# A linear-attention and mixture-of-experts kernel: one ordered attention block with its own beginning, shorter angle arithmetic, one power for two norms, scatters ahead of state sums, shared steps of the first sequence four tiles sooner

## The chip, the cores and the metric

The kernel runs on one core of a Trainium2 chip. The metric is the time of one execution on the device in microseconds (us). The engines are TensorE (PE, matrix products; PEld is its weight load), VectorE (DVE), ScalarE (ACT), GpSimd (POOL) and SyncE (SP, which issues most DMAs). Each engine takes its own instructions in order; they meet through semaphores.

## The reference

The input x has 16 sequences of 512 tokens of 128 features. Two layers follow each other, each with a residual and a layer norm behind it.

```
q, k, v = silu(x @ Wq), silu(x @ Wk), x @ Wv        # 16 heads of 8
q, k    = [t*cos(theta*n), t*sin(theta*n)]          # n is the position, per head
out     = ((q k^T) * lower_triangle) v              # no softmax
out     = (out @ Wo) * sigmoid(x @ G1 @ G2)
x       = layernorm(x + (layernorm of out)*gamma + beta)

probs   = softmax(rmsnorm(x) @ router^T)            # 8 experts, the best 2 of each token
routed  = sum over the 2 experts of w * (silu(xg @ rg) * (xg @ ru)) @ rd
          # an expert takes its first 1280 tokens in order
shared  = (silu(x @ sg) * (x @ su)) @ sd
x       = layernorm(x + shared + routed)
```

## The kernel before

**Tiles.** A tile is 128 tokens; there are 64, four to a sequence (NC = 4). Attention is done tile by tile with a running state per sequence, so a tile needs its own 128 by 128 energies and the state of the tiles before it.

**The beginning.** Positions come from iotas. The angles theta*n are reduced to whole turns in `angles` (L299 to L311, nine DVE instructions per chunk c): the number of turns is the product of `turns_of` and the position plus MAGIC (L304), MAGIC is taken off and the result multiplied with the two parts of two pi (L305, L308), and the difference is put together (L307, L309), its size taken (L310) and it is clamped (L311). `sines` (L316 to L326) has ACT take cosine and sine of a chunk in four instructions, into `cst_tok`; `same` (L331) copies half of it. The four chunks serve all sequences.

**One attention tile t.** `project` (L414): two products with the weights into a PSUM tile `pq`, three Silu on ACT into `qk` (L425, L427), a Tanh for the gate (L433), four ACT copies that spread the values into `vpad` (L441), and on DVE the product of `qk` with the sines, `hat` (L445). `turn_over` (L452): four transposes of `hat` on PE, and four ACT instructions that bring them back (L460, L465, L467). `energies` (L493): 32 products, masked by four DVE instructions (L513). `values` (L518): products with the state and the values; ACT brings the result to `oT` (L544). `remember` (L470): the products of keys and values, masked by DVE (L488), and added to the running state by POOL (L490). All their PSUM tiles but the energies are of one tag, "w", with four buffers.

**After a sequence.** `after(b)` (L547) is a generator: the output product, the gate, a layer norm, a residual, a second layer norm, the transpose into `x1T` and the router's logits. Its reciprocal roots are powers on POOL (L113 through `rstd_of`); L591 to L594 work out the reciprocal root for the router's norm from the second norm. `route(b0, b1)` (L618) is a generator over a group of sequences (0 to 5, 6 to 11, 12 to 15) of small DVE instructions, an Exp, two counting products, and it fills a list of 128 scatters. A scatter (L723) is an indirect DMA on POOL that writes the rows of one tile to an expert's slots. `scatter_behind` (L736) puts an optional small POOL product, `beat` (L740), ahead of it, which makes POOL wait for a given column.

**The shared network** is a list `feed` of 384 steps (`shared_order`, L182): per sequence 16 gate or up steps of one product of 512 columns each (L137, L150), and 8 down steps of four products (L160). A gate step has a Silu on ACT (L139), an up step a product on DVE (L151), every second down step a sum on DVE (L165). A sequence's steps may start when `ready[b]` allows.

**What sets the order.** Blocks under `tc.manual_schedule(engines=ORDERED)` keep the written order on PE, ACT, DVE and POOL. Before, there are three such blocks in the attention phase: the set-up (L217), the first angles with the masks (L333), and the main loop (L788). Each keeps its own order, and the scheduler interleaves them. The main loop runs t from -2 to 64; in each pass it does `project(t+2)`, a shared step, some steps of `route`, `turn_over(t+1)`, a shared step, a step of `after`, `energies(t)`, `values(t-1)`, `remember(t+1)`, two scatters, and more steps of `after` and `route`. `beginning(t)` (L389) puts the later angles and sines ahead of `project`. A tail loop follows with one shared step per pass and a scatter in every second one. Then come the experts (L999), and a final loop (L1047 to L1066), which takes a shared step per pass, and beside it sums the experts' rows (`add_up`, every second pass) and deals out steps of the last layer norm (`finish_lot`, three steps for two passes), in lots of four tiles, and of one tile for the last four. When the shared steps are used up, what is left of these runs by itself.

Of the kernel before, what the change touches and what calls it, by code (L numbers as in the profile page):

```python
# [10 lines left out]
F32 = mybir.dt.float32  # L11
I32 = mybir.dt.int32
AF = mybir.ActivationFunctionType
ALU = mybir.AluOpType
# [33 lines left out]
def tile_kernel(  # L48
# [44 lines left out]
    rms = keep.tile([P, NT], F32, name="rms")  # L93
# [101 lines left out]
    with ExitStack() as ph:  # L195
# [21 lines left out]
        with tc.manual_schedule(engines=ORDERED):  # L217
            th_row = cst.tile([1, D + HALF], F32, name="th_row")
            nc.sync.dma_start(th_row, theta.unsqueeze(0))
# [15 lines left out]
            nc.vector.memset(half_pi, math.pi / 2)  # L235
            warm = cst.tile([P, 1], F32, name="warm")
# [36 lines left out]
            for vp in vpads[:2]:  # L273
                nc.gpsimd.memset(vp, 0.0)

            def nought(tile_, n):
                nc.scalar.copy(tile_, zcol.to_broadcast([P, n]))

            pth = ps_w.tile([P, D + HALF], F32, tag="w", name="pth")
            nc.tensor.matmul(pth, ones[0:1, :], th_row, start=True, stop=True)  # L280
            th_sb = wk1.tile([P, D + HALF], F32, tag="w", name="th_sb")
            nc.scalar.copy(th_sb, pth)
# [3 lines left out]
            for vp in vpads[2:]:  # L286
                nought(vp.rearrange("p a b d -> p (a b d)"), 640)
# [3 lines left out]

            cst_tok = cst.tile([P, NC, 2, 16, 2, 8], F32, name="cst_tok")
            scratch = hp.tile([P, 10, D + HALF], F32, tag="h", name="scratch")
            turns_of = wk1.tile([P, D + HALF], F32, tag="o", name="turns_of")
            nc.vector.tensor_scalar(turns_of, pth, 1.0 / (2.0 * math.pi), None, ALU.mult)

        def angles(c, th):  # L299

            a, size, k, whole = scratch[:, c], scratch[:, NC + c], scratch[:, 8], scratch[:, 9]
            both = ((slice(0, D), pos[:, 0, c : c + 1]), (slice(D, D + HALF), pos[:, 1, c : c + 1]))
            for m, at in both:
                nc.vector.tensor_scalar(k[:, m], turns_of[:, m], at, MAGIC, ALU.mult, ALU.add)  # L304
            nc.vector.tensor_scalar(whole, k, MAGIC, -C1, ALU.subtract, ALU.mult)  # L305
            for m, at in both:
                nc.vector.scalar_tensor_tensor(a[:, m], th[:, m], at, whole[:, m], ALU.mult, ALU.add)  # L307
            nc.vector.tensor_scalar(k, k, MAGIC, -C2, ALU.subtract, ALU.mult)  # L308
            nc.vector.tensor_tensor(a, a, k, ALU.add)  # L309
            nc.vector.scalar_tensor_tensor(size, a, -1.0, a, ALU.mult, ALU.max)  # L310
            nc.vector.tensor_scalar(a, a, -PI_BELOW, PI_BELOW, ALU.max, ALU.min)  # L311
# [4 lines left out]
        def sines(c):  # L316

            for s, (from_, scale, bias) in enumerate([(scratch[:, NC + c], -1.0, half_pi), (scratch[:, c], 1.0, 0.0)]):
                nc.scalar.activation(
                    cst_tok[:, c, 0, :, s, :], from_[:, 0:D].rearrange("p (h d) -> p h d", d=8), AF.Sin,  # L320
                    scale=scale, bias=bias,
                )
                nc.scalar.activation(
                    by_twos(cst_tok[:, c, 1])[:, :, 1, :, s, :],
                    from_[:, D:].rearrange("p (a i d) -> p a i d", i=2, d=8), AF.Sin, scale=scale, bias=bias,
                )  # L326

        def same(c):

            to, of = (by_twos(cst_tok[:, c, a])[:, :, 0].rearrange("p a i s d -> p a (i s d)") for a in (1, 0))  # L330
            nc.vector.tensor_copy(to, of)  # L331

        with tc.manual_schedule(engines=ORDERED):  # L333
            angles(0, pth)
            sines(0)
            angles(1, th_sb)
            same(0)

# [3 lines left out]
            nc.gpsimd.tensor_tensor(causal[:, 0:1], scratch[:, 0, 0:1], zcol, ALU.mult)  # L342
# [13 lines left out]
            for at in (0, HALF):  # L356
                rows = causal[at : at + HALF, :]
                nc.gpsimd.affine_select(
                    rows, rows, pattern=[[1, HALF]], compare_op=ALU.is_ge, fill=0.0, base=0, channel_multiplier=-1
                )  # L360
            expi = cst.tile([P, E], I32, name="expi")
# [27 lines left out]
        def beginning(t):  # L389

            if t == -1:
                sines(1)
            elif t == 0:
                angles(2, th_sb)
                sines(2)
            elif t == 1:
                angles(3, th_sb)
                sines(3)

# [14 lines left out]
        def project(t):  # L414

            b, c = divmod(t, NC)
            pq = ps_w.tile([P, 16, 32], F32, tag="w", name=f"pq_{t}")
# [6 lines left out]
            qk = wk2.tile([P, 2 * D], F32, tag="qk", name=f"qk_{t}")  # L424
            nc.scalar.activation(qk[:, 0:D].rearrange("p (h d) -> p h d", d=8), pq[:, :, 0:8], AF.Silu)  # L425
            for u in range(2):
                nc.scalar.activation(  # L427
                    qk[:, D:].rearrange("p (a u i d) -> p a u i d", u=2, i=2, d=8)[:, :, u],
                    pq[:, 0:8, 16 + 8 * u : 24 + 8 * u].rearrange("p (a i) d -> p a i d", i=2), AF.Silu,
                )  # L430
            if c == 0:
                gates[b] = wk2.tile([P, NC, D], F32, tag="gate", name=f"gate_{b}")
# [3 lines left out]

            vp, v = vpads[t % NVP], pq[:, 8:16, 16:32].rearrange("p k (u d) -> p k u d", u=2)
# [4 lines left out]
            if 0 < t < NC:  # L442
                same(t)
# [103 lines left out]
        def after(b):  # L547
# [28 lines left out]
            r2 = rstd_of(mv2[:, :, 1], NC, LN_EPS)  # L576
# [12 lines left out]

            sq = small.tile([P, NC], F32, tag="sq", name="sq")  # L590
            nc.vector.tensor_tensor(sq, r2, r2, ALU.mult)  # L591
            nc.vector.tensor_tensor(sq, sq, mv2[:, :, 1], ALU.mult)
            nc.vector.tensor_scalar(sq, sq, RMS_EPS, None, ALU.add)
            nc.gpsimd.tensor_tensor(rms[:, mine], sq, neghalf[:, :NC], ALU.pow)  # L594
# [193 lines left out]
        with tc.manual_schedule(engines=ORDERED):  # L788
            for t in range(-2, NT + 1):
                coming, here, left = 0 <= t + 2 < NT, 0 <= t < NT, 0 <= t - 1 < NT  # L790
                stopped("wait")
                beginning(t)
# [5 lines left out]
                if t == 0:  # L798
                    nc.vector.tensor_scalar(wo_sb, wo_sb, 0.5, None, ALU.mult)
# [16 lines left out]
                if 0 <= t + 1 < NT:  # L816
                    remember(t + 1)
                if left:

                    scatter_behind(oTs[(t - 1) // NC][:, ds((t - 1) % NC * P, 1)])  # L820
                    scatter_behind()
                advance(turns, "narrow")
# [3 lines left out]
                if left and (t - 1) % NC == NC - 1:  # L826
                    b = (t - 1) // NC
                    turns.append(after(b))
                    ready[b] = t + (6 if b else 10)
                    for b0, b1 in groups:  # L830
                        if b == b1 - 1:
                            todo.append((b, route(b0, b1)))
# [5 lines left out]
            while turns or todo or scatters or fills or over:  # L838
# [17 lines left out]
                t += 1  # L856

# [255 lines left out]
```

## Time and profile before

| | us |
|---|---|
| median of 8 runs (lowest, highest) | 856.41 (854.03, 857.22) |
| the profiled execution | 852.86 |
| its span, first to last instruction | 851.2 |

| stretch of the span, us | what runs | PE busy |
|---|---|---|
| 9.53 to 35.86 | tiles 0 to 6 of attention | 19.96 of 26.33 |
| 80.55 to 102.64 | attention with shared steps | 22.09 of 22.09 |
| 355 to 510 | tail loop: shared steps and scatters | 152.94 of 155 |
| 510 to 750 | experts | 238.05 of 240 |
| 750 to 843 | final loop | 89.56 of 93 |
| 843 to 851.2 | the last layer norms alone | 0 |

Matrix products are pipelined, so a busy PE holds some waiting inside; the table shows where it stands still. The timeline of an engine gives for each group of instructions its start, its duration, and in brackets the time that the engine stood idle before it and what ended that time. The starts of L445, one per tile, mark the pace of the attention phase; "hat 6" in what follows is the seventh of them.

### The profile page before, as it was taken

The numbers are of one execution on the slowest core, as the hardware profiler recorded it, in microseconds if no ns is written. First come the engines' busy times: TensorE is split into PE (matmuls) and PEld (weight loads), VectorE is DVE, ScalarE is ACT, GpSimd is POOL, SyncE is SP. The second block draws the span as 40 slices with busy tenths as digits, with TensorE's granted clock in tenths as the row PEclk, the third lists the DMA queues.
The fourth block names the chain that finished last, engine by engine and source line by source line (L and its number), as shares of the span: only waits on it lengthen the run. The fifth ranks groups of instructions, "written<-read, shape, count | busy, mean of one in ns | idle before, by whom it ended". The sixth has DMA issues, their size and how long they took to land. (4 is left out here: it accounts for less than half of the span.)

```text
span 851.2 us, 25793 instructions
## 1 busy us (share of the span) xinstructions
PE 814.0 (96%) x10288; PEld 555.6 (65%) x10288; DVE 538.8 (63%) x1695; ACT 413.7 (49%) x1342; POOL 360.1 (42%) x512
## 2 busy tenths in 40 slices
PE   6899999989999999999999999999999999999995
PEld 4666667656766765755666666776777667765564
DVE  8688887889988788975433334443434443278864
ACT  5676776675676667434222221333333333323455
POOL 2233333322366767686766660433343333401110
PEclk9899999999999999999999999999999999999998
DMA  6011111111021110067000014212331110056412
GB/s 202 22 36 34 35 33 35 34 34 29 27 58 57 56 48 25 26 215 247 28 11 7 2 37 134 84 35 91 94 98 55 62 59 25 31 161 180 143 49 63
DMA packets 66395, 57.55 MB, mean 68 GB/s; under 512 B 6180, under 2 KB 55132, under 8 KB 66274
## 3 DMA queue, kind: packets, MB, share of 16 engines
q1 hardware_dynamic: 59474, 44.95, 17.3%
q0 software_dynamic: 6656, 10.69, 3.8%
q8 instruction: 81, 1.33, 0.7%
q14 instruction: 40, 0.33, 0.1%
q10 hardware_dynamic: 144, 0.26, 0.1%
HBM read 32.62 MB, written 26.48 MB: 69 GB/s over the span
## 5 line engine op out<-in xcount | busy, mean ns | idle before, releaser
L723 POOL DMA_INDIRECT xg_dram<-x,idx x128 | 128.6, 1004 | 40.4 <-issue 35.1
L934 POOL DMA_INDIRECT y_dram<-y,to x80 | 77.5, 969 | 158.2 <-ACT y L932 158.2
L151 DVE TENSOR_TENSOR h<-sl,pu 128x512 f32<-128x512 f32 x128 | 87.7, 685 | 84.5 <-PE pu L150 56.3
L139 ACT ACTIVATE sl<-pg 128x512 f32<-128x512 f32 x128 | 75.5, 593 | 118.1 <-PE pg L137 112.5
L150 PE MATMUL pu<-x1T,su_sb 128*128 128x512 f32 x256 | 131.0, 593 | 0.7 <-ACT sl L139 0.7
L137 PE MATMUL pg<-x1T,sg_sb 128*128 128x512 f32 x256 | 131.4, 595 | 0.0
L160 PE MATMUL pd<-sd_sb,h 128*128 128x128 f32 x1024 | 122.8, 276 | 4.4 <-DVE x1T L165 4.4
L1026 DVE TENSOR_TENSOR eh<-esl,peu 128x512 f32<-128x512 f32 (+1 forms) x96 | 57.5, 599 | 109.7 <-PE peu L1023 109.7
L160 PEld LDWEIGHTS pd<-sd_sb,h 128*128 128x128 f32 x1024 | 119.1, 192 | 11.3 <-issue 5.7
L113 POOL TENSOR_TENSOR rstd<-ve,neghalf 128x4 f32<-128x4 f32 x45 | 48.6, 1080 | 124.7 <-DVE ve L111 119.8
L928 PEld LDWEIGHTS ped<-rd,eh 128*128 128x128 f32 x640 | 84.1, 192 | 24.6 <-issue 22.5
L490 POOL TENSOR_TENSOR state<-state,add 128x128 f32<-128x128 f32 x96 | 44.0, 458 | 129.9 <-DVE add L488 127.3
L513 DVE TENSOR_TENSOR et<-pe,causal 128x256 f32<-128x256 f32 x256 | 90.4, 417 | 8.8 <-PE pe L505 8.7
L1021 PE MATMUL peg<-xgT,rg 128*128 128x512 f32 (+1 forms) x192 | 84.6, 523 | 0.0
L1023 PE MATMUL peu<-xgT,ru 128*128 128x512 f32 (+1 forms) x192 | 84.4, 521 | 0.0
L928 PE MATMUL ped<-rd,eh 128*128 128x128 f32 x640 | 84.4, 275 | 0.0
L1025 ACT ACTIVATE esl<-peg 128x512 f32<-128x512 f32 (+1 forms) x96 | 50.5, 526 | 55.0 <-PE peg L1021 52.3
L150 PEld LDWEIGHTS pu<-x1T,su_sb 128*128 128x128 f32 x256 | 45.8, 190 | 45.1 <-issue 39.0
L932 ACT ACTIVATE y<-ped,wt 128x128 f32<-128x128 f32 x80 | 29.4, 367 | 84.6 <-PE ped L928 84.6
L137 PEld LDWEIGHTS pg<-x1T,sg_sb 128*128 128x128 f32 x256 | 44.5, 191 | 36.8 <-issue 34.8
L418 PE MATMUL pq<-W,xT 128*128 128x384 f32 x128 | 61.0, 560 | 5.4 <-ACT qT L467 2.0
L445 DVE TENSOR_TENSOR hat<-qk,cst_tok 128x512 f32<-128x512 f32 x64 | 45.0, 703 | 25.8 <-ACT qk L427 25.7
(176 smaller groups left out, 1259.8 us busy)
## 6 DMA issues: line engine op xcount, KB each, us to landing
y_dram<-vpad SPq DMA_DIRECT2D x16, 512.0 KB, 7.0
y<-y_dram SPq DMA_DIRECT2D x32, 256.0 KB, 3.2
xT<-xt SPq DMA_DIRECT2D x15, 384.0 KB, 3.1
xg<-xg_dram SPq DMA_DIRECT2D x8, 660.0 KB, 4.4
x<-x SPq DMA_DIRECT2D x16, 256.0 KB, 3.4
o<-res SPq DMA_DIRECT2D x15, 256.0 KB, 2.3
xg_dram<-x,idx POOLq DMA_INDIRECT x128, 2.3
rg<-rg SPq DMA_DIRECT2D x8, 256.0 KB, 4.7
```

The lines of the kernel that those rows point to most:

```text
L137: nc.tensor.matmul(pg, sg_sb[:, ts(i, P)], seq, start=True, stop=True)
L139: nc.scalar.activation(sl, pg, AF.Silu)
L150: nc.tensor.matmul(pu, su_sb[:, ts(i, P)], seq, start=True, stop=True)
L151: nc.vector.tensor_tensor(h[i // half][:, i % half, :], h.pop(("s", i)), pu, ALU.mult)
L160: nc.tensor.matmul(pd, h[k][:, i - k * half, ts(c, P)], sd_sb[:, i, :], start=(i == 0), stop=(i == IS // P - 1))
L418: nc.tensor.matmul(pq[:, :, 0:24], xts[b][:, c, 0:P], W[:, 0:384].rearrange("p (h n) -> p h n", n=24), start=True, stop=True)
L513: nc.vector.tensor_tensor(et.rearrange("p s i n -> p (s i) n"), pes[a, half].rearrange("p s i n -> p (s i) n"), causal.unsqueeze(1).to_bro ...
L723: i = nc.gpsimd.indirect_dma_start(out=xg_dram[:, :], out_offset=bass.IndirectOffsetOnAxis(ap=idx[:, k, t : t + 1], axis=0), in_=x1[:, t, ...
L928: nc.tensor.matmul(pd, h[:, i, ts(c, P)], got[e][2][:, i, :], start=(i == 0), stop=(i == IR // P - 1))
L934: i = nc.gpsimd.indirect_dma_start(out=y_dram[:, :], out_offset=bass.IndirectOffsetOnAxis(ap=to[:, at : at + 1], axis=0), in_=y, in_offset ...
L1021: nc.tensor.matmul(pg[:, :n], rg_sb[:, ts(i, P)], xgTs[e][:, ds(o0, n)], start=True, stop=True)
L1023: nc.tensor.matmul(pu[:, :n], ru_sb[:, ts(i, P)], xgTs[e][:, ds(o0, n)], start=True, stop=True)
```

## The change

- **One ordered block.** The set-up, the first angles and the main loop are one ordered block. The work of tiles 0 to 2 is written out by hand, and the loop starts at t = 1. `project` is cut into `products`, `squash`, `gate`, `spread` and `turn`, so that these can be placed singly.
- **Angles.** The product of theta with the position goes to ACT (`linear`, eight instructions), the number of turns comes from a matrix product with a row of 1/(2 pi), and `angles` has six DVE instructions. The size is taken by ACT (Abs) at the head of `sines`.
- **Loads and memsets.** theta is loaded by ACT's queue ahead of the weights. Two of the four `vpad` tiles, which ACT filled with noughts, are cleared by DVE and by POOL.
- **Norms.** `after` works out both reciprocal roots by one power over eight columns.
- **Scatters** stand ahead of `remember` in the pass.
- **Shared steps** of sequence 0 may start at t = 10 instead of t = 14.

The diff, cut to its core:

```diff
-    rms = keep.tile([P, NT], F32, name="rms")
+    norms = keep.tile([P, 2, NT], F32, name="norms")
+    rms = norms[:, 1]
...
-        with tc.manual_schedule(engines=ORDERED):
+        ordered = ExitStack()
+        ordered.enter_context(tc.manual_schedule(engines=ORDERED))
+        if True:
             th_row = cst.tile([1, D + HALF], F32, name="th_row")
-            nc.sync.dma_start(th_row, theta.unsqueeze(0))
+            nc.scalar.dma_start(th_row, theta.unsqueeze(0))
...
+            by_turn = cst.tile([1, P], F32, name="by_turn")
+            nc.vector.memset(by_turn, 1.0 / (2.0 * math.pi))
...
+            nc.vector.memset(vpads[3], 0.0)
...
+            pth = ps_w.tile([P, 2, M], F32, tag="w", name="pth")
+            nc.tensor.matmul(pth[:, 0], ones[0:1, :], th_row, start=True, stop=True)
+            nc.tensor.matmul(pth[:, 1], by_turn, th_row, start=True, stop=True)
...
-            for vp in vpads[2:]:
-                nought(vp.rearrange("p a b d -> p (a b d)"), 640)
...
+            def linear(c):
+                for m, order in both:
+                    nc.scalar.activation(
+                        scratch[:, NC + c, m], pth[:, 0, m], AF.Copy, scale=pos[:, order, c : c + 1]
+                    )
+
+            linear(0)
+            linear(1)
+            nc.scalar.copy(turns_of, pth[:, 1])
...
+            for c in range(2, NC):
+                linear(c)
+
+        def angles(c, turns):
+
+            a, k = scratch[:, c], scratch[:, 8 + c % 2]
+            for m, order in both:
+                nc.vector.tensor_scalar(a[:, m], turns[:, m], pos[:, order, c : c + 1], MAGIC, ALU.mult, ALU.add)
+            nc.vector.tensor_scalar(k, a, MAGIC, None, ALU.subtract)
+            nc.vector.scalar_tensor_tensor(a, k, -C1, scratch[:, NC + c], ALU.mult, ALU.add)
+            nc.vector.scalar_tensor_tensor(a, k, -C2, a, ALU.mult, ALU.add)
+            nc.vector.tensor_scalar(k, a, -PI_BELOW, PI_BELOW, ALU.max, ALU.min)
...
         def sines(c):
+            nc.scalar.activation(scratch[:, NC + c], scratch[:, c], AF.Abs)
...
+            nc.gpsimd.memset(vpads[2], 0.0)
...
+            ve = small.tile([P, 2, NC], F32, tag="ve2", name="ve2")
+            nc.vector.tensor_scalar(ve[:, 0], mv2[:, :, 1], LN_EPS, None, ALU.add)
+            inv = small.tile([P, NC], F32, tag="sq", name="inv")
+            nc.vector.reciprocal(inv, ve[:, 0])
+            nc.vector.tensor_tensor(inv, inv, mv2[:, :, 1], ALU.mult)
+            nc.vector.tensor_scalar(ve[:, 1], inv, RMS_EPS, None, ALU.add)
+            nc.gpsimd.tensor_tensor(
+                norms[:, :, mine], ve, neghalf[:, : 2 * NC].rearrange("p (k c) -> p k c", k=2), ALU.pow
+            )
...
-            sq = small.tile([P, NC], F32, tag="sq", name="sq")
-            nc.vector.tensor_tensor(sq, r2, r2, ALU.mult)
-            nc.vector.tensor_tensor(sq, sq, mv2[:, :, 1], ALU.mult)
-            nc.vector.tensor_scalar(sq, sq, RMS_EPS, None, ALU.add)
-            nc.gpsimd.tensor_tensor(rms[:, mine], sq, neghalf[:, :NC], ALU.pow)
...
+            products(0)
+            products(1)
+            sines(0)
+            squash(0)
+            turn(0)
+            spread(0)
+            gate(0)
+            sines(1)
+            turn_over(0)
+            angles(2, turns_of)
+            remember(0)
+            squash(1)
+            turn(1)
+            spread(1)
+            gate(1)
+            energies(0)
+            products(2)
+            turn_over(1)
+            remember(1)
+            angles(3, turns_of)
+            sines(2)
+            squash(2)
+            turn(2)
+            spread(2)
+            gate(2)
+            nc.vector.tensor_scalar(wo_sb, wo_sb, 0.5, None, ALU.mult)
+            for t in range(1, NT + 1):
...
                 if left:
                     values(t - 1)
+                if left:
+
+                    scatter_behind(oTs[(t - 1) // NC][:, ds((t - 1) % NC * P, 1)])
+                    scatter_behind()
                 if 0 <= t + 1 < NT:
                     remember(t + 1)
-                if left:
-
-                    scatter_behind(oTs[(t - 1) // NC][:, ds((t - 1) % NC * P, 1)])
-                    scatter_behind()
...
-                    ready[b] = t + (6 if b else 10)
+                    ready[b] = t + 6
```

## The prediction

> **What bounds the kernel now.** I read the page's head, then the timeline of the first 36 us, then the busy times of chosen stretches, then the timeline of the end.
>
> ```profile
> span 851.2 us, 25793 instructions
> PE 814.0 (96%) x10288; PEld 555.6 (65%) x10288; DVE 538.8 (63%) x1695; ACT 413.7 (49%) x1342; POOL 360.1 (42%) x512
> PEclk9899999999999999999999999999999999999998
> ```
>
> PE is full almost everywhere. The clock row dips only in the second slice and at the end. So time is lost at the two ends, and a step moved between full stretches gains nothing.
>
> ```profile
> 1.86 1.34 DVE L258 CAST pos<-posj 128x4 f32<-128x4 int32 x1 [0.29 <-POOL posj L257]
> 1.97 1.21 POOL L274 MEMSET vpad<- 128x640 f32 x2
> ...
> 14.41 0.40 ACT L319 ACTIVATE cst_tok<-scratch,half_pi 128x128 f32<-128x128 f32 x1 [1.63 <-DVE scratch L310]
> ...
> 16.52 1.65 PE L418 MATMUL pq<-W,xT 128*128 128x384 f32 x2 [1.99 <-ACT vpad L441]
> ...
> 21.09 0.40 ACT L319 ACTIVATE cst_tok<-scratch,half_pi 128x128 f32<-128x128 f32 x1 [3.23 <-DVE scratch L310]
> ...
> 23.20 0.68 PE L479 MATMUL pst<-vpad,hat 64*32 64x64 f32 x30 [2.07 <-ACT vpad L441]
> 24.59 1.65 PE L418 MATMUL pq<-W,xT 128*128 128x384 f32 x2 [0.72 <-ACT qT L467]
> ...
> 30.34 0.91 PE L418 MATMUL pq<-W,xT 128*128 128x384 f32 x2
> ```
>
> Columns are start, duration, engine, line, names, and the idle time before. In the beginning ACT stands 1.63 and 3.23 us for the angles of chunks 2 and 3; PE then stands 1.99 and 2.07 us for ACT to free a PSUM buffer. The same two matmuls take 1.65 us after these waits and 0.91 us at 30.34: the clock had been halved.
>
> ```profile
> 9.53:35.86 26.33, 19.96 (x468) 14.28 (x476) 18.18 (x60) 16.28 (x80) 4.47 (x15) 0.81 0.28 93
> 62.16:80.55 18.39, 16.45 (x475) 11.83 (x460) 15.73 (x59) 13.14 (x60) 7.41 (x10) 1.00 0.13 39
> 80.55:102.64 22.09, 22.09 (x494) 14.07 (x493) 18.39 (x63) 15.53 (x64) 7.35 (x10) 1.00 0.12 33
> 748.77:804.07 55.30, 52.23 (x263) 34.98 (x262) 45.60 (x145) 20.89 (x46) 8.08 (x8) 1.00 0.59 170
> 804.07:842.67 38.60, 38.56 (x186) 24.99 (x184) 24.55 (x93) 21.11 (x47) 5.51 (x5) 1.00 0.19 55
> 842.67:851.20 8.53, 0.00 (x0) 0.00 (x0) 3.12 (x17) 4.06 (x12) 0.00 (x0) 0.68 0.21 62
> ```
>
> Each row: stretch, length, busy time of PE, PEld, DVE, ACT, POOL, then clock. The first runs from hat 0 to hat 6 (starts of L445), the second over four tiles without steps of the shared network, the third over four tiles with eight. The last three are the final loop and the 8.5 us after PE's last product.
>
> ```profile
> 842.37 1.65 ACT L988 ACTIVATE res<-x1T,nb,rstd 128x128 f32<-128x128 f32 x4 [0.44 <-DVE nb L985]
> 842.67 0.29 DVE L165 TENSOR_TENSOR x1T<-pd,x 128x128 f32<-128x128 f32 x1 [0.34 <-PE pd L160]
> 843.92 0.28 ACT L119 ACTIVATE root<-mv,eps_col 128x1 f32<-128x1 f32 x1
> 848.13 0.49 ACT L988 ACTIVATE res<-x1T,nb,rstd 128x128 f32<-128x128 f32 x1 [0.47 <-ACT root L119]
> ```
>
> Behind the last sum (842.67) four tiles are normed one by one.
>
> **Part 1, the beginning.** Angles fall from nine DVE instructions to six: by the rows two of L304 (0.20 from start to start), then L305 0.26, two of L307/L310's kind 0.36 and 0.38, L311 0.28, together 1.7 us against 2.4. ACT gains eight linear products (0.17 to 0.20 each, by L282's and L427's rows), all before 6 us, and loses two nought copies (1.35) and th_sb. It gains four Abs. No row shows Abs: 0.32 by L282 (128x192 copy), between 0.24 (L323) and 0.40 (L319); I take 0.34. The vpad memsets go to DVE (0.17 per 128 columns by L231, so about 0.6, before the angles) and POOL (0.64).
>
> ACT's queue in the new order, by start-to-start rows (squash 0.38, spread 0.65, gate 0.16, the four copies of a turn-over 1.26, sines 0.90 plus Abs 0.34): linears from 3.9 to 5.9, sines(0) to 7.1, squash, spread and gate of 0 to 8.3, sines(1) to 9.6, turn-over 0 to 10.8, tile 1 to 12.0, then a wait of about 1.3 for PE's transposes of hat 1 (behind products(2)), turn-over 1 to 14.6, sines(2) to 15.8, tiles 2 and 3 to 18.2, sines(3) to 19.5. The angles are done long before each. So hats fall at 7.9, 11.4, 16.2, 19.6, 22.5, 26.1, 30.0. Laid end to end in the same way, with four PSUM buffers and full clock, the old order gives 9.4, 10.6, 15.5, 21.9, 25.8, 29.3, 33.3; the trace has 9.53, 10.74, 15.81, 22.49, 27.31, 32.81, 35.86. Order alone is worth 3.3 us at hat 6; the half clock cost the old one 2.6 more. PE still idles near 15 us in the new order, so I let it recover a third of that: **-4.2**, bounds -3.0 and -5.9. From hat 6 on both run alike.
>
> The Trainium skill speaks to two steps here. The row first: the two 128x4 DVE operations at 1.86 and 2.08 last until POOL's memset ends at 3.18. SBUF — State Buffer, section "SBUF: two separate sides", calls the pair of ports shared by VectorE and GpSimd an exclusive lock held for a whole instruction; by it POOL's new memset, which falls among the angles or hat 0, could add its 0.64 us, and the sum would be -2.6 instead of -3.2. ScalarE: Activation LUTs, section "Table sets: the hidden batching unit", lists abs as filler in every set, so it expects no table load; no run here shows Abs yet.
>
> **Part 2, shared steps of sequence 0 from t=10, not t=14.** Counting the program's order: of 384 steps the main loop now takes 102, the tail loop 164, then 4, and the final loop 114; with the change 110, 164, 4 and 106. Eight steps (0.86 by L137, 0.89 by L160) leave the final loop: -7.0. Four tiles of the main loop go from the second window row to the third: 22.09 - 18.39 = +3.7. But the final loop deals out one and a half closing steps per shared step. Twelve fewer are dealt: behind the last sum stand, beside the four single tiles, three more res, a whole lot (four stats, root, nb, four res) and an nb queued behind the last sum on DVE. From the last sum: nb at +0.45, four res to +2.4 (1.65 by the row), root to +2.7, reciprocal and nb to +3.2, four res to +4.8, and then the first single root, which now comes at 843.92 - 842.67 = +1.25: **+3.5**. While sums are added (748.77 to 804.07) DVE is 82% busy and PE lost 55.30 - 52.23 = 3.1; the shift puts six more gate/up steps there in place of downs (0.685 against 0.286 per two steps, so +1.2 of DVE), and gate/up steps instead of downs around the wait for xg near 511 to 519: +1.0, bounds -0.7 and +2.2. Part 2: -7.0 + 3.7 + 3.5 + 1.0 = **+1.2**.
>
> The shift also moves downs against the two bursts of routing (hats 34 to 40 and 58 to 63; the six tiles from 181.90 to 218.86 took 36.96 us against 1.5 times 22.09, so 3.8 more). Hats 33 to 36 get downs, 37 to 40 get gate/ups: 0, bounds -2.0 and +3.2.
>
> **Part 3, one power for both norms.** DVE loses L591, L592, L593 (0.33 + 0.22 + 0.27) and gains a reciprocal (0.17 by L121), a product and a sum (0.22 + 0.17): -0.3 per sequence, hidden behind PE. POOL loses L594 (1.04); the one power has 8 columns: between 1.04 (L113) and 2.08 (twice it), I take 1.5. The mean/rstd product L580 waits for it on DVE, with h and the next hat behind it; at 53.33 the power ended 0.75 us before L580 started, so a chain 0.4 + 0.5 longer just fits. **-0.2**, bounds -0.6 and +1.0.
>
> **Part 4, scatters before state sums.** The scatters (two of 1.0 us and a beat of 0.2) start when oT is copied instead of after POOL's sum; the sums (0.45 each) come 2.2 us later, and are read by values two tiles later, over 5 us on. What was late there, POOL's power, ends no later. 0, bounds -0.5 and +0.5.
>
> **Sum:** -4.2 + 1.2 - 0.2 = -3.2. The profiled execution took 852.86 with a span of 851.2, so 849.7; it lay 3.55 under the median of the eight runs (856.41), from which the same step gives **853.2**.
>
> **Rivals.**
> - *The clock holds and the moved steps hide.* PE at full clock through the beginning (-5.9), part 2 at its low bound (-0.5): -6.5, 850.0. For it: the loss is a mean clock of 0.81 over 26.33 us, 5 us' worth, tied to waits that the order removes; against: PE's idle time near 15 us.
> - *The gain is given back.* Beginning -3.0, part 2 at +2.4, nothing else: -0.6, 855.8. For it: the static queue at the end leaves no choice.
> - *Slower:* gate/up steps meet the routing bursts. From 201.03 to 208.06 DVE is busy 6.89 of 7.03 us; with +0.4 per tile for eight tiles PE waits 3.2 us more. With the beginning at -3.0 and part 2 at +2.4 the sum is +2.6, 859.0; it decides once the shift costs 2.3 at these bounds, or 4.9 with the other terms as forecast. Against: the same DVE work leaves hats 33 to 36.
> - *A table load at each Abs and back* would be eight times the 1.28 us of L644's load on ACT's chain: +10.3 - 3.2, 863.5. It is counted with the slower ones.
>
> **Numbers.** Forecast 0.50, clock rival 0.20, given back 0.20, slower 0.10 (0.02 of it the table load). The range takes in the clock rival and the given-back one with the runs' scatter: 849.0 to 857.0. A measurement of this kernel can tell about 0.2% (1.7 us) from no change: faster 0.70, same 0.20, slower 0.10.
>
> **What would show it.** Right: no ACT wait on scratch after 10 us, hat 6 near 30 to 32.5, the first shared product near 57 us (79.8 - 18.4 - 4.2), and more than 8.5 us (near 12) behind PE's last product. Wrong: a table load beside Abs; PE waiting longer than before near hats 37 to 40; hat 6 after 33.5; a final loop with over 4 us of PE waits.

## The result and the profile after

The changed kernel took 865.29 us (median of 7 runs, 862.99 to 866.90), the kernel before 854.7 beside it (20 runs): ratio 1.0122, 95% interval 1.0108 to 1.0136, so 9.2 to 11.6 us slower. The forecast was 853.2, with 849.0 to 857.0 as its range: wrong in sign. The profiled execution took 866.38 with a span of 864.6. Starts of the same instruction in both profiles, with the sum that the forecast's own steps give at that place:

| mark, us from the span's start | before | after | difference | forecast |
|---|---|---|---|---|
| hat 0 | 9.53 | 10.33 | +0.80 | -1.6 |
| hat 6 | 35.86 | 35.24 | -0.62 | -4.2 |
| hat 16 | 80.55 | 84.97 | +4.41 | -0.5 |
| hat 63 | 351.35 | 359.90 | +8.55 | -0.7 |
| last scatter | 507.03 | 516.98 | +9.95 | -0.7 |
| first product on ept (experts) | 520.83 | 536.79 | +15.96 | -0.7 or a little more |
| PE's last product ends | 842.63 | 852.47 | +9.84 | -6.7 |
| end | 851.15 | 864.57 | +13.42 | -3.2 |

The table says at once where to look: the beginning gave little, the main loop lost all the way down, the wait before the experts lost 6 more, and the last two stretches (-6.1 and +3.6) did what was forecast. The page of the kernel after:

```profile
span 864.6 us, 25765 instructions
...
PE 819.2 (95%) x10290; PEld 555.7 (64%) x10290; DVE 536.2 (62%) x1682; ACT 416.8 (48%) x1353; POOL 357.3 (41%) x496
...
PEclk9899999999999999999999998999999999999998
```

PE's work grew from 814.0 to 819.2 though it has only the small product with 1/(2 pi) more; DVE and POOL have less. A new dip of the clock stands in the 25th slice (519 to 540 us), ahead of the experts. The stretches that answer to those of before, with the same columns:

```profile
10.33:35.24 24.91, 20.34 (x468) 14.62 (x475) 16.37 (x53) 17.84 (x84) 4.80 (x16) 0.86 0.27 85
62.18:84.97 22.79, 22.40 (x494) 14.07 (x493) 18.69 (x64) 15.56 (x64) 6.99 (x9) 1.00 0.11 32
84.97:107.67 22.70, 22.32 (x494) 14.06 (x493) 18.67 (x63) 15.55 (x63) 6.99 (x9) 1.00 0.11 32
757.74:813.04 55.30, 52.08 (x265) 34.96 (x264) 40.89 (x126) 19.52 (x43) 8.22 (x9) 1.00 0.55 160
852.47:864.60 12.13, 0.00 (x0) 0.00 (x0) 5.18 (x29) 6.34 (x18) 0.00 (x0) 0.68 0.22 65
```

Four tiles with shared steps took 22.09 before and 22.70 now, with the same products on PE: 0.61 us per sequence that PE does not need. The end is as forecast (12.13 us behind PE's last product), and its timeline shows the two whole lots ahead of the single tiles:

```profile
852.51 0.29 DVE L166 TENSOR_TENSOR x1T<-pd,x 128x128 f32<-128x128 f32 x1 [0.29 <-PE pd L161]
...
853.11 1.65 ACT L1044 ACTIVATE res<-x1T,nb,rstd 128x128 f32<-128x128 f32 x4 [0.57 <-DVE nb L1041]
...
855.50 1.65 ACT L1044 ACTIVATE res<-x1T,nb,rstd 128x128 f32<-128x128 f32 x4 [0.49 <-DVE nb L1041]
857.06 0.28 ACT L120 ACTIVATE root<-mv,eps_col 128x1 f32<-128x1 f32 x1
```

One thing has to be known for the rest. The kernel before has two levels of time, from one set of runs to another: 854.7, 854.67 and 855.42 us in three sets, 865.32, 866.43 and 865.04 in three others, and two of the chips showed both. Each experiment is compared with the kernel before of its own set.

| set: kernel before | kernels, median us (ratio, 95%) |
|---|---|
| 1: 854.67 | a_ready10 861.36 (1.0059 to 1.0097), a_oldnorms 856.88 (1.0014 to 1.0041), a_clearlate 863.04 (1.0080 to 1.0114), a_pth2 864.02 (1.0084 to 1.0122) |
| 2: 865.32 | n_ops 865.78 (1.0000 to 1.0021), n_pow8 858.38 (0.9908 to 0.9939), a_begin 855.71 (0.9883 to 0.9920), best 854.80 (0.9850 to 0.9893) |
| 3: 866.43 | b_again 866.71 (0.9994 to 1.0012), best_again 853.66 (0.9829 to 0.9863), b_ready6 869.88 (1.0024 to 1.0050), best_scback 861.48 (0.9931 to 0.9960) |
| 4: 855.42 | b_scfirst 855.32 (0.9987 to 1.0008), a_again 866.11 (1.0105 to 1.0149), b_norms 862.47 (1.0067 to 1.0098), best_third 850.57 (0.9930 to 0.9964) |
| 5: 865.04 | a_begin_2 855.93 (0.9879 to 0.9916), a_norms_shift 873.69 (1.0086 to 1.0127) |

### The profile page after: what moved, and what is told of

It is laid out like the page before. It is cut to its first block, busy times and chain, and to the rows that moved or that the text cites. A ratio compares the mean times of both kernels' runs of the same rounds, so it can differ in the third digit from the quotient of the medians.

```text
span 864.6 us, 25765 instructions
## 1 busy us (share of the span) xinstructions
PE 819.2 (95%) x10290; PEld 555.7 (64%) x10290; DVE 536.2 (62%) x1682; ACT 416.8 (48%) x1353; POOL 357.3 (41%) x496
## 5 line engine op out<-in xcount | busy, mean ns | idle before, releaser
L138 PE MATMUL pg<-x1T,sg_sb 128*128 128x512 f32 x256 | 133.4, 603 | 0.9 <-DVE h L152 0.9
L517 POOL TENSOR_TENSOR state<-state,add 128x128 f32<-128x128 f32 x96 | 46.5, 484 | 108.3 <-DVE add L515 105.4
L114 POOL TENSOR_TENSOR rstd<-ve,neghalf 128x4 f32<-128x4 f32 x28 | 28.6, 1021 | 116.4 <-DVE ve L112 110.1
L472 DVE TENSOR_TENSOR hat<-qk,cst_tok 128x512 f32<-128x512 f32 x64 | 52.4, 818 | 36.0 <-ACT qk L444 35.6
```

The lines of the kernel that those rows point to most:

```text
L138: nc.tensor.matmul(pg, sg_sb[:, ts(i, P)], seq, start=True, stop=True)
```

## The experiments

### The one power: its place on DVE

In both kernels the statistics of the second norm stand on DVE just ahead of a hat. DVE before, then DVE after, at the same place of sequence 2:

```profile
91.80 0.36 DVE L107 BATCH_NORM_AGGREGATE mv<-st 128x2 f32<-128x6 f32 x4
92.19 0.17 DVE L111 TENSOR_SCALAR ve<-mv 128x4 f32<-128x4 f32 x1
92.27 0.68 DVE L445 TENSOR_TENSOR hat<-qk,cst_tok 128x512 f32<-128x512 f32 x1
...
95.93 0.31 DVE L593 TENSOR_SCALAR sq<-sq 128x4 f32<-128x4 f32 x1
96.68 0.69 DVE L445 TENSOR_TENSOR hat<-qk,cst_tok 128x512 f32<-128x512 f32 x1 [0.43 <-ACT qk L427]
```

```profile
96.61 0.17 DVE L605 TENSOR_SCALAR ve<-mv 128x4 f32<-128x4 f32 x1
96.81 0.18 DVE L607 RECIPROCAL inv<-ve 128x4 f32<-128x4 f32 x1
97.03 0.16 DVE L608 TENSOR_TENSOR inv<-inv,mv 128x4 f32<-128x4 f32 x1
97.22 0.17 DVE L609 TENSOR_SCALAR ve<-inv 128x4 f32<-128x4 f32 x1
97.30 0.68 DVE L472 TENSOR_TENSOR hat<-qk,cst_tok 128x512 f32<-128x512 f32 x1
```

The reader is to see the missing bracket. The hat at 92.27 has no idle time before it: DVE is what it waits for, so whatever is put ahead of it moves the tile. The hat at 96.68 stood idle for 0.43 us for ACT; the old three operations stood ahead of that one, in time that nobody needed. Now the hat starts 0.69 behind the sum with eps (97.30 - 96.61) instead of 0.08: 0.61 more.

**a_oldnorms** takes the change's norms back:

```diff
-            nc.vector.tensor_scalar(ve[:, 0], mv2[:, :, 1], LN_EPS, None, ALU.add)
...
-            r2 = norms[:, 0, mine]
+            r2 = rstd_of(mv2[:, :, 1], NC, LN_EPS)
...
+            nc.vector.tensor_tensor(sq, r2, r2, ALU.mult)
+            nc.vector.tensor_tensor(sq, sq, mv2[:, :, 1], ALU.mult)
+            nc.vector.tensor_scalar(sq, sq, RMS_EPS, None, ALU.add)
+            nc.gpsimd.tensor_tensor(rms[:, mine], sq, neghalf[:, :NC], ALU.pow)
```

> The changed kernel with the old two powers per sequence and the three DVE operations of sq behind the first two normed rows again. My theory: the four new DVE operations stand ahead of the next hat on DVE and delay it by 0.6 us a sequence, of which about 0.35 is kept; over the main loop 4 us: about 861 us, hat 63 near 356 instead of 359.9, with the interval before the hat that follows the second norm's statistics back from 6.0 to 5.4. Rival (the amount of DVE work counts, not its place: the new form is 0.3 us shorter): same time or slower, 865 to 867.

Measured: 856.88, so 8.4 us under the changed kernel, twice what was expected; hat 16 to hat 20 takes 22.09 again. The theory's place was right and its "about 0.35 is kept" wrong: nearly all is kept.

**n_ops** and **n_pow8** start from a_oldnorms, with `rstd_of` written out, and put back one suspect each (the lines that make the tiles are left out here). n_ops, whose three results nobody reads:

```diff
             nc.vector.tensor_scalar(ve, mv2[:, :, 1], LN_EPS, None, ALU.add)
+            nc.vector.reciprocal(inv, ve)
+            nc.vector.tensor_tensor(inv, inv, mv2[:, :, 1], ALU.mult)
+            nc.vector.tensor_scalar(inv, inv, RMS_EPS, None, ALU.add)
             nc.gpsimd.tensor_tensor(r2, ve, neghalf[:, :NC], ALU.pow)
```

> The changed kernel with the old two powers (as in a_oldnorms) and, in addition, three DVE operations of 128x4 whose results nobody reads, in the place where the changed kernel has its reciprocal, product and second sum: behind the sum with eps, ahead of the power and of the next hat. It tells the place of the DVE operations from the wider power. My theory: the place costs. Each of the 16 sequences starts the next hat 0.61 us later (three times 0.20 from start to start), and little of that comes back: main loop longer by 6 to 8 us than in a_oldnorms, about 864 beside 856.9. Rival (the power of 8 columns, 2.02 us instead of 1.04, delays the mean/rstd product and what queues behind it): within 1 us of a_oldnorms, 857 to 858.

n_pow8:

```diff
-            nc.vector.tensor_scalar(ve, mv2[:, :, 1], LN_EPS, None, ALU.add)
...
-            nc.gpsimd.tensor_tensor(r2, ve, neghalf[:, :NC], ALU.pow)
+            nc.vector.tensor_scalar(ve8, mv2[:, :, 1].unsqueeze(1).to_broadcast([P, 2, NC]), LN_EPS, None, ALU.add)
...
+            nc.gpsimd.tensor_tensor(r8, ve8, neghalf[:, : 2 * NC].rearrange("p (k c) -> p k c", k=2), ALU.pow)
+            r2 = r8[:, 0]
```

> The changed kernel with the old two powers (as in a_oldnorms), the first of them made 8 columns wide (both halves the same), with no DVE operation more. My theory: the wider power is hidden, since the mean/rstd product starts some 3 us behind it: within 1 us of a_oldnorms, 857 to 858. Rival (the wider power is what the new norms cost): 861 to 864.

Measured in one set: 865.78 and 858.38. Three operations of 0.17 us in that place cost 7.4 us (hat 16 to hat 20 takes 22.70 in n_ops, 22.09 in n_pow8); the power of 8 columns is hidden.

**b_norms** is the kernel before with the one power alone.

> The kernel before with the one power for both norms as the only edit. Theory: the three DVE operations ahead of the next hat cost 0.6 us a sequence, as n_ops showed in the changed kernel: 6 to 8 us slower than the kernel before beside it. Rival (the norms cost only together with the shift or the scatters): within 2 us of the kernel before.

Measured: 862.47 beside 855.42, +7.1. The one power needs no other part of the change to cost this.

### The earlier shared steps

**a_ready10** gives sequence 0 its old due time:

```diff
-                    ready[b] = t + 6
+                    ready[b] = t + (6 if b else 10)
```

> The changed kernel with the shared steps of sequence 0 due from t=10+4=14 again, as in the kernel before; all else stays changed. My theory: three of the four terms of the shift go back: hats from 16 on come 3.7 us earlier, the final loop gets 6.1 longer, the tail 3.6 shorter, and the gate/up steps leave the wait for xg before the experts, which gets 6.0 shorter. Sum -7.2: about 858 us beside 865.3 of the changed kernel. Rival A (the wait for xg grew because of the scatters' new place or the new norms, not because of which steps stand in it): the wait stays at 19.8 us from the last scatter to the first product on ept, and the sum is -1.2, about 864. Rival B (the shift also collides with the routing bursts): more than -8.

Measured: 861.36, so -3.9 and not -7.2; the first theory's sum was too large, and rival A's too small. **b_ready6** is the converse, the kernel before with `ready[b] = t + 6`:

> The kernel before with sequence 0 due from t=10 as its only edit. Theory, from the difference that a_oldnorms showed behind hat 12: main loop +1.9 us, wait for xg +6, final loop -6.1, tail +3.5, sum about +5.3: 860. Rival (the shift costs only together with the new norms or with the scatters' new place): within 1.5 us of the kernel before, or my forecast of +1.2.

Measured: 869.88 beside b_again's 866.71, +3.2, between theory and forecast. The terms, from profiles of the same set (b_ready6 against b_again) and of the changed kernel against a_ready10:

| term, us | forecast | b_ready6 - b_again | after - a_ready10 |
|---|---|---|---|
| hat 12 to 16 | +3.7 | +3.8 | +3.8 |
| hat 16 to 63 (with both routing bursts) | 0 | -2.0 | -2.6 |
| hat 63 to the first product on ept | part of +1.0 | +4.2 | +3.7 |
| ept to PE's end | -7.0, part of +1.0 | -6.1 | -6.1 |
| PE's end to the end | +3.5 | +3.3 | +3.2 |
| sum from hat 12 | +1.2 | +3.2 | +2.0 |

The two profiles of the last column lie 4.05 apart at the end, and 2.09 of it lie before hat 12, where nothing differs: the chance of the clock, below. Chance has a part in the -2.6 too: from hat 34 to 36 a_ready10 ran at a mean clock of 0.87, the changed kernel at 1.00. The term that fails is the wait before the experts: from the last scatter to the first product on ept it took 19.81 us in b_ready6 and in the changed kernel, 13.79 in b_again and 16.07 in a_ready10. The timeline of the kernel after there, DVE and PE:

```profile
526.06 1.67 DVE L949 TENSOR_TENSOR xg<-xg,ok 128x528 int32<-128x528 int32 x3 [4.70 <-DMA xg<-xg_dram]
527.65 1.28 DVE L152 TENSOR_TENSOR h<-sl,pu 128x512 f32<-128x512 f32 x2
...
528.39 1.36 PE L151 MATMUL pu<-x1T,su_sb 128*128 128x512 f32 x2 [3.06 <-DVE h L152]
...
530.60 2.08 PE L138 MATMUL pg<-x1T,sg_sb 128*128 128x512 f32 x2 [0.85 <-DVE h L152]
...
534.18 1.91 PE L138 MATMUL pg<-x1T,sg_sb 128*128 128x512 f32 x2
```

DVE stands at `clear_rows` (L949) until the expert's rows have landed; the products of the up steps queue behind it; PE runs out of PSUM buffers and stands for 3.06 and 0.85 us; and then its clock is halved, so that the next products take 1.91 to 2.08 instead of 1.02. Before, downs stand in this place; their sums on DVE queue in the same way, but PE stood only 1.37 us and its clock held:

```profile
517.23 2.05 PE L160 MATMUL pd<-sd_sb,h 128*128 128x128 f32 x16 [1.37 <-DVE x1T L165]
```

In a_ready10, with downs in this place again, PE stood 1.98 us and the same 16 products took 3.68: so what the wait costs depends on the clock too.

**a_clearlate** puts the three `clear_rows` of expert 0 behind the four shared steps:

```diff
-            for o0, n in parts:
-                clear_rows(0, o0, n)
             for _ in range(4):
                 feed.pop(0)[2]()
+            for o0, n in parts:
+                clear_rows(0, o0, n)
```

> The changed kernel in which the three clear_rows of expert 0 stand behind the four shared steps instead of ahead of them; nothing else moves. My theory: the 6.0 us lost at the wait for xg come from gate/up steps whose DVE products queue behind the clear_rows that waits for the transfer; with the clear behind them PE works through the steps at once, and only the transposes wait for the rows: first ept product near 532 instead of 536.8, sum -4.5, about 861. Rival (the transfer itself lands late and sets the time): PE's gap only moves behind the steps, -1 to 0, about 865.

Measured: ept 532.86 as expected, 863.04 instead of 861. From the last scatter to ept the time is 15.56 instead of 19.81, so the queue on DVE was the cause of 4.25 of the 6.0 us. Of the rest a part is the transfer: in the changed kernel `clear_rows` began 9.08 us behind the last scatter, before 7.87; why isn't shown. But from the experts' last product to PE's end it took 96.32 instead of 94.73 us, with a stretch at half clock that the changed kernel's profile lacks (there the same 32 products took 3.84 behind a wait of 1.88). PE in a_clearlate, a down group of 32 products at the common speed and one behind a wait:

```profile
799.77 3.73 PE L161 MATMUL pd<-sd_sb,h 128*128 128x128 f32 x32
805.37 5.47 PE L161 MATMUL pd<-sd_sb,h 128*128 128x128 f32 x32 [1.87 <-DVE x1T L166]
```

**a_norms_shift** has both edits, the one power and the due time, on the kernel before.

> The kernel before with the one power and the due time of 10 for sequence 0, without the new beginning and without the scatters' new place. Theory: the two prices add up, 7.1 for the norms and 3.5 to 5 for the shift: 866 beside 854.7 to 855.4, ratio 1.012 to 1.015. Rival (each hides part of the other): 862 to 864.

Measured: 873.69 beside 865.04, +8.7 (7.4 to 11.0). That is in the band of the rival (+7 to +9), but 7.1 + 3.2 = 10.3 lies inside the interval too, so the run doesn't decide whether one part hides some of the other.

### The beginning

Timeline of the kernel after:

```profile
1.86 0.17 DVE L263 CAST pos<-posj 128x4 f32<-128x4 int32 x1 [0.29 <-POOL posj L262]
...
6.34 0.54 DVE L320 TENSOR_SCALAR scratch<-pth,pos 128x128 f32<-128x128 f32 x2 [2.97 <-ACT scratch L302]
...
8.06 0.36 ACT L331 ACTIVATE scratch<-scratch 128x192 f32<-128x192 f32 x1 [1.75 <-DVE scratch L323]
...
11.17 1.08 PE L485 MATMUL pt<-ident,hat 128*128 128x128 f32 x4 [1.96 <-DVE hat L472]
...
14.54 1.65 PE L432 MATMUL pq<-W,xT 128*128 128x384 f32 x2
...
21.60 1.09 PE L485 MATMUL pt<-ident,hat 128*128 128x128 f32 x4 [2.25 <-DVE wo_sb L846]
```

The first angle instruction, which reads half of `pth`, waits 2.97 us for ACT, which reads the other half: both are in one PSUM tile, and the program has DVE wait for the last of ACT's eight linear products. So hat 0 falls at 10.33, not 7.9, PE stands 1.96 and 2.25 us, and products take 1.65 instead of 0.91. Abs (L331) took 0.36 with no table load beside it.

**a_pth2** gives the second product a bank of its own, and puts ACT's copy out of it ahead of the linear products; which of the two does more isn't separated:

```diff
+            ptu = ps_e.tile([P, M], F32, tag="e", name="ptu")
+            nc.tensor.matmul(ptu, by_turn, th_row, start=True, stop=True)
...
+            nc.scalar.copy(turns_of, ptu)
             linear(0)
             linear(1)
-            nc.scalar.copy(turns_of, pth[:, 1])
...
-            angles(0, pth[:, 1])
+            angles(0, ptu)
```

> The changed kernel with the product of theta and 1/(2 pi) in a PSUM bank of its own, and its copy ahead of the linear products on ACT; nothing else moves. My theory: the first angle instruction no longer waits for all ACT products on the shared tile (6.34 us) but for one copy (near 4.4), so hat 0 comes 1.5 to 2 us earlier, hat 6 by 1 to 2: about 864. Rival (PE's halved clock and its order set hat 6): hat 0 earlier, hat 6 within 0.5 us, 865.

Measured: 864.02. DVE in its profile:

```profile
3.53 0.54 DVE L321 TENSOR_SCALAR scratch<-ptu,pos 128x128 f32<-128x128 f32 x2 [0.16 <-ACT turns_of L307]
...
7.72 0.69 DVE L473 TENSOR_TENSOR hat<-qk,cst_tok 128x512 f32<-128x512 f32 x1 [0.17 <-ACT qk L445]
```

The angles start 2.81 us earlier and hat 0 falls at 7.72, where the forecast had put it (7.9). PSUM — Partial Sum Buffer in the Trainium skill, section "PSUM bank collisions raise a hardware error", says to guard PSUM by bank and not by address; the wait at 6.34 and its going at 3.53 agree with a program built in that way.

Hat 6 differs from execution to execution of one and the same beginning, so it takes many profiles: old beginning 35.9 (mean of six, 35.43 to 36.71), the change's 34.2 (nine, 33.16 to 35.71), with a bank of its own 31.1 (five, 29.91 to 31.73). So at hat 6 the change's beginning is worth -1.7, and with the bank -4.9. Of the bank's 3.1 the medians keep 1.3 (a_pth2 beside the changed kernel) and 0.9 (best beside a_begin, below); where the rest goes isn't shown.

**a_begin** keeps of the change the beginning and the scatters' place (due time and powers old), **best** adds the bank:

> The changed kernel with sequence 0 due from t=14 and the old two powers again: what is left of the change is its beginning and the scatters ahead of the sums. My theory: hat 6 comes 0.6 to 2.7 us earlier than in the kernel before, and from there on both run alike: faster by 0.6 to 2.7 us, ratio 0.997 to 0.999. Rival (the new beginning or the place of the scatters costs something later): ratio 1.000 or more.

> As a_begin, and the product of theta and 1/(2 pi) in a PSUM bank of its own (as in a_pth2). My theory: hat 6 comes 4.8 us earlier than in the kernel before, as in a_pth2, and nothing of it is given back, since the shared steps and the norms stand as before: ratio 0.994 to 0.995, about 850. Rival (the early part of the gain is lost at the routing bursts or at the wait for xg, which follow the scatters and not the hats): ratio 0.997 or more.

Measured 855.71 and 854.80, in a set where the kernel before took 865.32: far too good for a beginning. The next runs were made for that.

### The two levels, and the scatters

> The kernel before, unchanged, as a run of its own. In one set of runs it took 865.3 us where it otherwise takes 853 to 857, on a chip where four other kernels showed small stops of TensorE near 365 us that the first chip did not show. If that is the chip, the profile shows where: more stops of this kind, or stretches at half clock (each up to 2 us). If the time is 853 to 857, the ratios of that set are to be read among its own kernels only.

**best_scback** is best with the scatters behind the state sums:

```diff
-                if left:
-                    scatter_behind(oTs[(t - 1) // NC][:, ds((t - 1) % NC * P, 1)])
-                    scatter_behind()
                 if 0 <= t + 1 < NT:
                     remember(t + 1)
+                if left:
+                    scatter_behind(oTs[(t - 1) // NC][:, ds((t - 1) % NC * P, 1)])
+                    scatter_behind()
```

> As best, with the scatters behind the sums of states again, as in the kernel before. My theory: the place of the scatters is worth nothing: within 1 us of best. Rival (the sums come later on POOL behind two scatters, and the products that read them wait at the end of the routing bursts): 1 to 3 us faster than best.

> The version with the new beginning, its second product in a bank of its own, the old due time and the old powers (label best), again. Theory: 851 to 853 against 854.7 of the kernel before; what the beginning gains (4.1 us at hat 6) is partly lost in stretches at half clock behind PE's waits of 1.9 us at the two routing bursts (1 to 1.4 us each). Rival (nothing is lost, the other set's chip was to blame): 850.

Measured in one set: before 866.43, b_again 866.71, best_scback 861.48, best_again 853.66. So the scatters' place was worth 7.8 us there, against my theory, and the level comes with the set of runs: set 3 ran on the chip of set 1. Where the time lies, PE and POOL before (first profile), then the same tile in b_again:

```profile
248.36 0.97 POOL L723 DMA_INDIRECT xg_dram<-x,idx  x1 [0.30 <-issue]
248.50 0.32 PE L530 MATMUL pout<-qT,state 128*32 128x64 f32 x8
...
248.97 0.44 PE L538 MATMUL pout<-et,vpad 128*32 128x64 f32 x16
249.34 0.45 PE L479 MATMUL pst<-vpad,hat 64*32 64x64 f32 x32
```

```profile
250.90 0.97 POOL L723 DMA_INDIRECT xg_dram<-x,idx  x1 [0.30 <-issue]
251.31 0.32 PE L530 MATMUL pout<-qT,state 128*32 128x64 f32 x8
251.44 0.50 PE L538 MATMUL pout<-et,vpad 128*32 128x64 f32 x6
252.37 0.39 PE L538 MATMUL pout<-et,vpad 128*32 128x64 f32 x10 [0.42 <-issue]
...
253.03 0.46 PE L479 MATMUL pst<-vpad,hat 64*32 64x64 f32 x32
```

In b_again PE stops inside the 16 products on et and vpad, and the profile names nothing that it waits for. From the first product on the state to pst it takes 1.72 us instead of 0.84 (248.50 to 249.34 before). From 200 to 400 us b_again has 14 such stops of 0.25 us or more and best_scback 15, all in the products of `values`; ten of the 14 end within 0.25 us ahead of the first DMA of a scatter just issued (here 252.45). Fourteen times 0.88 us is 12.3, and from hat 20 to the last scatter b_again falls 13.2 us further behind the first profile. The first profile has no such stop, though there too the first DMA of 17 scatters falls beside such products; so the tie to the scatters is argued from the places, not shown. best_again has 3 and a_begin 3, all behind 362 us: with the scatters ahead of the sums the first DMA of 9 scatters instead of 25 falls beside these products (best_again, b_again).

> The kernel before with its scatters ahead of the state sums as the only edit. Theory: in sets of runs where the kernel before takes 865 to 867 us, TensorE stops for 0.4 us inside the products on et and vpad whenever a scatter is being issued beside them (14 stops between 230 and 380 us, each costing near 0.85 us); the new place puts TensorE at other products then, so 8 to 10 us faster, near 856. Where the kernel before takes 854.7, no such stop is there to take away: 0. Rival (my step: the place of the scatters is worth nothing in either): within 1 us of the kernel before in any set.

> The changed kernel, unchanged. It has its scatters ahead of the sums, so it should take 864 to 867 us in any set of runs, whatever the kernel before takes beside it. Rival (the slower sets add to every kernel): 870 or more where the kernel before takes 866.

> The version labelled best, a third time, beside the others of this set. Theory: 852 to 855 in any set, so 2 us under the kernel before at most where that takes 854.7, and 12 under it where it takes 866.

Measured, with the kernel before at 855.42: b_scfirst 855.32, a_again 866.11, best_third 850.57. No stop in any of the three profiles. Where the stops are missing the scatters' place is worth nothing, as forecast, and the changed kernel is 10.7 us slower. best_third beats both kernels: 0.53% under the kernel before, 1.8% under the changed one (850.57 / 866.11). It differs from b_scfirst by the beginning with the bank alone, and lies 4.75 under it: this prices a beginning such as the prediction had meant (-4.2). With the kernel before at 865.04:

> The version with the new beginning and the scatters ahead of the sums, and the old due time and old powers, again, beside a kernel before that I hope to see at 854 to 856. It prices my part 1, forecast -4.2. Theory from hat 6 in the profiles (0.6 to 2.7 us earlier): 1 to 2.5 us faster than the kernel before. Rival (the forecast's -4.2 holds once the other parts are gone): 4 us faster or more.

Measured: 855.93. That set had the stops (the kernel of a_norms_shift has 15), so this run tells of the scatters again and could not price the beginning.

What makes the stops come in one set of runs and not in another isn't shown. The changed kernel itself was not run in a set that had them; n_ops, near to it, took 865.78 beside 865.32 there, so in such a set the change would cost next to nothing, by this estimate: the scatters' place would pay for the rest.

## Why the prediction was wrong

- **"-0.3 per sequence, hidden behind PE" (part 3).** This is the step that failed: +7.1 alone, 8.4 within the change, instead of -0.2. I weighed the power's delay against the mean/rstd product, and that was right (n_pow8), but counted DVE's operations by their sum and not by their place. The removed ones stood ahead of a hat that waited for ACT, the added ones ahead of a hat that waited for DVE.
- **"+1.0, bounds -0.7 and +2.2" (part 2, DVE in the final loop and the wait for xg).** The mechanism was named and its size wrong: 3.7 to 4.2 from hat 63 to the first product on ept. I priced DVE's extra work (0.685 against 0.286), not the queue behind an instruction that waits for a transfer, nor the half clock behind PE's wait. The other terms held: +3.8 for +3.7, +3.2 for +3.5, -6.1 for -7.0 with what I had set against it.
- **"0, bounds -2.0 and +3.2" for the routing bursts.** -2.0 to -2.6. The gate/up steps did cost something where the slower rival had them: hats 38 to 42 took 1.8 us longer in both pairs of the table. But hats 34 to 38 took 2.0 and 3.1 less, with downs there, so the sum has the other sign, and slower came from elsewhere.
- **"-4.2" for the beginning (part 1).** -1.7, with hat 6 at 35.24, behind the 33.5 named as a sign of being wrong. The order was worked out rightly (with the bank hat 0 is at 7.72 and hat 6 earlier by 4.9), but I let DVE and ACT read one PSUM tile side by side. Before, too, DVE's L297 starts at 3.58, just behind ACT's copy of the same tile (3.17, for 0.32).
- **0 for the scatters (part 4).** Right in the sets like the first, 8 us wrong in the others.
- **No table load at Abs, about 12 us behind PE's end, the first shared product early**: right in kind (0.36; 12.13; 61.37 instead of 57, and 57.18 in a_pth2).
- **Two slips that change nothing.** The clock rival's terms add up to -6.4, not -6.5; and of the two DVE operations held beside POOL's first memset, the one at 2.08 is of 128x1, not 128x4.

The parts add up to -1.7 + 2.0 to 3.2 + 7.1 to 8.4 = 7.4 to 9.9, against 10.6 measured (9.2 to 11.6); the rest of 0.7 to 3.2 us is of the size of one or two stretches at half clock (1.25 to 1.7 us each, below), and isn't settled.

## What to carry to other kernels

An instruction on an engine with free time costs nothing only where it stands: look whether the next instruction that others wait for has idle time before it, and on whom. Before work is put beside a wait for a transfer, look which of its results go through the engine that stands at that wait. Run the kernel before again, in another set, before a difference of one per cent is put down to a change.

## What the runs showed of the hardware

- **Behind a wait of 1.9 us the clock falls in one execution and holds in another.** At the first routing burst PE stood for 1.90 us in before and in a_begin_2, and ran on with the same products, at 188.43 and at 186.63. The granted clock from 188 to 192 us (last column but two), before, then a_begin_2:

```profile
188.00:192.00 4.00, 3.57 (x117) 2.82 (x117) 3.61 (x11) 3.22 (x12) 0.20 (x1) 1.00 0.02 4
```

```profile
188.00:192.00 4.00, 4.00 (x110) 3.09 (x101) 2.71 (x9) 1.93 (x6) 0.69 (x2) 0.60 0.03 6
```

  The stretch costs 1.25 us here (3.65 us from the products into `pe` to those into `pq`, instead of 2.40) and 1.7 in a_clearlate (5.47 against 3.73, behind 1.87 us). TensorE: Matmul & The Clock Gate in the Trainium skill, section "What's actually happening", has the clock fall after an idle window of about 3.4 us, which runs freely and does not start with the kernel. That the outcome differs from run to run agrees; that 1.90 us of standing sufficed does not fit a whole idle window, and the measurement decides.
- **A hat beside POOL's additions takes longer.** In the changed kernel ten hats beside POOL's addition of bet (L581) took 1.30 to 1.52 us instead of 0.69, and eight beside the end of a scatter and the state sum (L517) behind it 0.84 to 0.99; before it was two hats, 1.31 and 1.02, beside the addition of bet. It shows in the group's mean, 818 ns against 703. Why the addition fell beside more hats isn't shown: with the wide power alone (n_pow8) it did so twice, as before. Between hats 16 and 20 it cost nothing, since n_ops, with no such hat there, needs the same 22.70. POOL's memset of 0.63 us did not do this to hat 0 (10.20 and 10.33). The rule on the shared ports that the prediction weighed (SBUF — State Buffer in the Trainium skill, section "SBUF: two separate sides") has a DVE instruction with two SBUF inputs held up only against a GpSimd instruction that reads SBUF; the hats, which have two inputs, agree: late beside the additions, on time beside the memset, which reads nothing. The cast of 128x4 at 1.86, which took 1.34 before and 0.17 now beside the same memsets of 1.21 us, stays open.
- **A power on POOL of twice the columns takes about twice as long**: 1.04 us for 4 (before, L113), 2.02 for 8 (after, L610; medians).
